# Two-level seven-product queries in the self-attention of a decoder layer

## The chip, the cores and the metric

The kernel runs on one core of one Trainium2 chip. The metric is the device time of one launch in microseconds (us), the median of several runs. A core has a matrix engine (PE, with its weight loads shown apart as PEld), a vector engine (DVE), a scalar engine (ACT), GpSimd (POOL) and a queue engine (SP) that here only issues DMAs. Each works through its own instructions in order; they wait for each other by semaphores.

## The reference

One decoder layer in float32, on x of 32 x 64 x 512, seen as 2048 tokens of 512 features: self-attention against a paged key and value cache, cross-attention against an encoded context, and a linear layer with eight low-rank experts. Each part is added to its input and layer-normalised.

```
x = layernorm(x + self_attention(x, wq, wk, wv, wo, caches, block_idx))
x = layernorm(x + cross_attention(x, context, Wq, bq, Wkv, bkv, Wo, bo))
x = layernorm(x + low_rank_experts(x, W, b, A, B, p_scores))

q = (x @ wq.T) -> 32 heads of 128          # rotary turn, one position for all
keys, values = 512 selected cache rows + 64 new ones, for each of 8 groups
attn = softmax(q . keys / sqrt(128)); out = (attn . values) @ wo.T
```

The change is in `q = x @ wq.T`. Eight key groups of four heads each share keys and values.

## The kernel before

Self-attention walks 128 *units*: key group g (8), token block tb (4 blocks of 512 tokens), head h (4). Four units of one group and block are a *block* b = n // 4; there are 32 blocks. The program order on PE, DVE and ACT is written out by hand; POOL's and SP's is left to a scheduler.

A unit handles four *tiles* i of 128 tokens. `scores` for a tile issues on PE two products of 288 keys each (L834) into one of two buffers; on DVE the row maximum `nmax` (L839); on ACT the exponential with the row sum (L842); on DVE the transposition of the tile before (`turn`, L865), the reciprocal of the sum (L851) and the scaling of p by it (L857; on ACT, L855, in some units). When the four tiles are done, `move` issues 16 DMAs on SP (L877) that bring the transposed p into `pT`. `values` of unit n - 2 (L885) runs on PE inside unit n: in an even unit two chunks, then two; in an odd unit three, then one and a pair of half chunks for both heads (`shared_values`), which ACT copies out (L908).

Between these stand *steps*: seven products q of the next block's queries, and seven products w of an earlier block's output projection. Each matrix of 512 x 512 is cut in four quarters and multiplied by the seven-product scheme (Winograd's form), one level deep: a product is 4 matmuls of 128 x 128 weights against 256 columns (`Product.mul`, L354). Products accumulate in PSUM, in the order 1, 2, 6, 7, 4, 5, 3: one product's sum must be read out of the bank before the next adds to it. The steps of a block stand at places 0 to 3 of its units by this line:

```
steps = {0: "qwqw", 1: "qw q", 2: "wqwq", 3: "w qw"}[h]
```

Place 0 is after the scores of tile 0, place 1 after the first part of `values`, place 2 after the scores of tile 2, place 3 after the second part of `values`. There are eight PSUM banks: two buffers of two banks for the scores, one bank for q, one for w, two for the values. So each q product, whatever its name (x, y, z), goes through the one q bank. ACT copies products 1 and 2 out (L383, L387); DVE adds the five others to the query matrix qT (L372, L395, L399). For w, DVE adds each product to the token sums `acc` (L553); product 1 has a second addition of twice the size (L561). In program order such a reading stands behind the tile's scaling.

POOL makes the operands: `token_sums` for the block's tokens (four subtractions of 128 x 512, L248 to L251), `load_left` for a group's wq (four, L242 to L245), `load_right` for wo (four), `output_sums` for w (four, L325 to L329), and two products of the rotation of the keys. The tokens of each block are loaded again from DRAM as four DMAs of 256 KB on SP (L120), for each of the eight groups.

The cross-attention further down already makes its queries in two levels: 49 products of 128 x 128 weights against 128 columns in two sets, of four and three outer products, 7 inner products each (`DeepQueries`, L493, read out by ACT at L504 to L511 and DVE at L501).

## Time and profile before

| | us |
|---|---|
| runs (three) | 3006.82, 3007.59, 3008.73 |
| median | 3007.59 |
| the profiled execution | 3004.51, of which 3002.7 is the span in the profile |
| PE busy | 2977.4 (99% of the span) |
| DVE busy | 2127.5 (71%) |
| POOL busy | 1218.9 (41%) |
| ACT busy | 1128.1 (38%) |
| granted PE clock | 0.999 of full speed |

The profile page gives busy times of each engine for one execution. A matmul row shows the time of one instruction until its modelled end; since they are pipelined, the rate is read from the distance between starts. One float32 matmul of the program is two PE instructions, so a product of four matmuls is eight. A row of groups gives busy us, mean ns of one, then the idle time of the engine before them and what ended it. The timeline gives the start, the time taken and the operation, runs of equal ones joined as xN.

### The profile page before, as it was taken

To read this page: it belongs to the slowest core of one execution; us is meant where nothing else is said; L and a number is where in the kernel's file an instruction comes from. 1 tells how busy PE (TensorE), PEld (TensorE's weight loads), DVE (VectorE), ACT (ScalarE), POOL (GpSimd) and SP (SyncE) were. 2 spreads that over 40 slices of the span, in tenths; PEclk is the share of its full clock that TensorE was granted. 3 is DMA by queue.
4 is the path that set the end of the run, shared out by engine and by line. 5 is a ranking of instruction groups with operands and counts; after the bars stand their busy time and mean duration, and the time that the engine had idled before them with its cause. 6 is when DMAs were issued, how large, how long until landed. Compare 5 with 4: busy or idle time off the path is not lost.

```text
span 3002.7 us, 46451 instructions
## 1 busy us (share of the span) xinstructions
PE 2977.4 (99%) x16144; PEld 2330.4 (78%) x16144; DVE 2127.5 (71%) x3907; ACT 1128.1 (38%) x2767; POOL 1218.9 (41%) x1024
## 2 busy tenths in 40 slices
PE   8999999999999999999999999999999999999998
PEld 6777777777777777777777768999999999999964
DVE  6787777777787777787787774636656666666686
ACT  4322223223223323323223232334455555555564
POOL 5222322321321321321321223667577577567532
PEclk9999999999999999999999999999999999999999
DMA  6554444444444444444444454666555455445420
GB/s 186 128 131 126 114 115 121 115 115 120 115 115 120 116 114 121 116 114 120 116 115 113 97 124 136 243 247 204 177 179 179 160 183 192 163 160 184 136 81 36
DMA packets 224042, 416.59 MB, mean 139 GB/s; under 512 B 48001, under 2 KB 103425, under 8 KB 215617
## 3 DMA queue, kind: packets, MB, share of 16 engines
q1 hardware_dynamic: 208720, 385.69, 45.0%
q0 software_dynamic: 4304, 19.01, 1.8%
q10 hardware_dynamic: 10784, 8.92, 1.0%
q8 instruction: 130, 2.13, 0.3%
q14 instruction: 104, 0.84, 0.1%
HBM read 206.60 MB, written 33.82 MB: 80 GB/s over the span
## 4 chain that ended last, share of the span: by engine, by line
PE 91%; DVE 3%; POOL 2%; SPq 2%; ACT 1%; DMA 1%; issue 0%; DVEq 0%; ACTq 0%; POOLq 0%
PE po L885 17%; PE s L834 16%; PE sx L1412 2%; PE pox L1495 2%; PE qx_1x L493 2%; PE qx_0x L493 2%; PE qx_2x L493 2%; PE qx_3x L493 2%; PE w_1y L354 1%; PE q_3y L354 1%; PE w_0y L354 1%; PE q_2y L354 1%; PE w_3y L354 1%; PE q_0y L354 1%; PE q_1y L354 1%; SPq L160 1%
## 5 line engine op out<-in xcount | busy, mean ns | idle before, releaser
L842 ACT ACTIVATE p<-s,nmax 128x576 f32<-128x576 f32 x512 | 379.1, 740 | 1210.7 <-DVE nmax L839 1155.4
L834 PE MATMUL s<-kT,qT 128*128 128x288 f32 x2048 | 574.7, 406 | 0.5 <-ACT p L842 0.5
L885 PE MATMUL po<-pT,v 128*128 128x512 f32 (+1 forms) x1280 | 549.0, 602 | 2.4 <-DMA acc<-in_x 1.9
L834 PEld LDWEIGHTS s<-kT,qT 128*128 128x128 f32 x2048 | 387.7, 190 | 100.6 <-issue 17.5
L839 DVE TENSOR_REDUCE nmax<-s 128x1 f32<-128x576 f32 x512 | 384.0, 750 | 58.6 <-PE s L834 57.2
L865 DVE STREAM_TRANSPOSE T<-p 128x576 f32<-128x576 f32 x512 | 394.4, 770 | 12.2 <-ACT p L855 7.4
L885 PEld LDWEIGHTS po<-pT,v 128*128 128x128 f32 (+1 forms) x1280 | 213.4, 189 | 202.0 <-issue 174.8
L857 DVE TENSOR_SCALAR p<-p,den 128x576 f32<-128x576 f32 x488 | 302.0, 619 | 17.1
L325 POOL TENSOR_TENSOR so<-oT,oT 128x512 f32<-128x512 f32 x32 | 40.7, 1272 | 545.3 <-ACT oT L908 545.2
L851 DVE RECIPROCAL den<-den 128x1 f32<-128x1 f32 x512 | 83.9, 164 | 224.8 <-ACT p L842 216.1
L328 POOL TENSOR_TENSOR so<-oT 128x512 f32<-128x512 f32 x32 | 40.7, 1271 | 310.3 <-PE w_1y L354 92.8
L249 POOL TENSOR_TENSOR tx<-xT 128x512 f32<-128x512 f32 x31 | 40.7, 1314 | 199.0 <-PE q_3z L354 63.3
L1444 ACT ACTIVATE exps<-exps,denx 128x64 f32<-128x64 f32 x480 | 121.0, 338 | 0.0
L1515 ACT ACTIVATE oTx<-pox,bv 128x128 f32<-128x128 f32 x248 | 71.1, 490 | 128.3 <-PE pox L1495 128.3
L325 POOL TENSOR_TENSOR sox<-oTx,oTx 128x512 f32<-128x512 f32 x31 | 39.3, 1269 | 149.0 <-DVE oTx L1517 132.4
L535 POOL TENSOR_TENSOR qTx<-d_in 128x512 f32<-128x512 f32 x68 | 85.1, 1274 | 34.7 <-ACT d_in L511 33.3
L842 ACT ACTIVATION_READ_ACCUMULATOR p<-s,nmax 128x1 f32 x512 | 98.7, 193 | 0.0
L535 POOL TENSOR_TENSOR qTx<-d 128x512 f32<-128x512 f32 x60 | 75.1, 1274 | 24.6 <-ACT d L511 23.2
L542 ACT ACTIVATE qTx<-qTx,bq 128x512 f32<-128x512 f32 x128 | 81.9, 713 | 0.0
L1517 DVE TENSOR_SCALAR oTx<-pox,bv 128x128 f32<-128x128 f32 x248 | 70.6, 425 | 14.2 <-PE pox L1495 14.2
L1412 PEld LDWEIGHTS sx<-kv_room,qTx 128*64 128x64 f32 x2048 | 62.3, 138 | 11.1 <-issue 10.1
L908 ACT COPY oT<-po 128x512 f32<-128x512 f32 x128 | 68.2, 587 | 4.1 <-PE po L885 3.8
(590 smaller groups left out, 6217.9 us busy)
## 6 DMA issues: line engine op xcount, KB each, us to landing
pT<-T SPq DMA_DIRECT2D x1016, 80.0 KB
pT<-T SPq DMA_DIRECT2D x1008, 64.0 KB
xT<-tl SPq DMA_DIRECT2D x28, 1792.0 KB
tlb<-tl SPq DMA_DIRECT2D x28, 1344.0 KB
xT<-in_xT SPq DMA_DIRECT2D x123, 256.0 KB
kv_room<-kv SPq DMA_DIRECT2D x32, 512.0 KB
pTx<-Tx SPq DMA_DIRECT2D x256, 64.0 KB
kv<-c SPq DMA_DIRECT2D x28, 512.0 KB
```

What stands on the lines that cost most here:

```text
L354: nc.tensor.matmul(self.banks[b][:, m, :], self.left[i][:, k, m * P : (m + 1) * P], self.right[i][:, k, :], start=(first and m + k == 0), ...
L493: nc.tensor.matmul(o[:, j, :], self.left[s][:, j, LEFT[i], :], self.right[s][:, j, RIGHT[i], :], start=(first and j == 0), stop=(j == len( ...
L535: nc.gpsimd.tensor_tensor(self.q[:, :, i, :, v, :], x.rearrange("p (o u) n -> p o u n", o=2), y.rearrange("p (o u) n -> p o u n", o=2), AL ...
L834: nc.tensor.matmul(s[:, a, :HALF], qTs[n // REP][:, units[n][2], i * P : (i + 1) * P], kTs[g][:, a * HALF : (a + 1) * HALF], start=True, s ...
L839: nc.vector.tensor_reduce(nmax, s[:, :, :HALF], AX.XY, ALU.max, negate=True)
L842: nc.scalar.activation(p.rearrange("q (a k) -> q a k", a=2), s[:, :, :HALF], AF.Exp, bias=nmax, accum_out=den,)
L851: nc.vector.reciprocal(den, den)
L857: nc.vector.tensor_scalar(p, p, den, None, ALU.mult)
L865: nc.vector.transpose(Ts[n][:, :, i, :], ps_.pop((n, i)).rearrange("q (b k) -> q b k", k=SQ))
L885: nc.tensor.matmul(pos[n].rearrange("d (a q) -> d a q", a=NQD), vs[units[n][0]][rows, v, :], pTs[n // 2][rows, :, chunk, :], skip_group_ch ...
L1412: nc.tensor.matmul(s[b * SEQ : (b + 1) * SEQ, i * REP + h, :], qTs[n][:, h, pr * HF + c0 : pr * HF + c0 + SEQ], kvs[n][:, pr, 0, c0 : c0 + ...
L1444: nc.scalar.activation(e[:, k, :], e[:, k, :], AF.Copy, scale=den[:, k : k + 1])
```

## The change

From the second key group on (blocks 4 to 31), the self-attention's queries are made in two levels, as 7 + 7 inner products: set 0 has four outer products (j = 0 to 3), set 1 three. A step of set 0 is four matmuls of 128 x 128 x 128, a step of set 1 three. The operands of the tokens do not depend on the group; POOL makes them once, in the first group, and they are kept in DRAM (`tq_all`) and loaded for every block into the new tile `tq`. The weights of a group are loaded in another layout (`wqD`) into the room of the old operands, and POOL makes the 49 parts of them. Block 0 to 3 keep the old products.

```
-            p = sb.tile([P, NKEY], F32, tag="p", name=f"p{u}", bufs=4)
+            p = sb.tile([P, NKEY], F32, tag="p", name=f"p{u}", bufs=3)
...
-            if n < REP or n >= N - REP and i % 2:
+            if n < REP or i % 2 and (n < 11 or n >= N - REP):
                 nc.scalar.activation(p, p, AF.Copy, scale=den)
...
+        SELF_ORDER = (1, 6, 7, 4, 5, 3, 2)
+            def step(self, s, i):
+                js = 4 - s
+                first = i in (1, 5, 2)
+                if first:
+                    self.bank = bank([P, 4, P], f"{self.name}_{s}{i}", "q")
+                o = self.bank
+                for j in range(js):
+                    nc.tensor.matmul(
+                        o[:, j, :], wdeep[s][:, j, LEFT[i], :], tq[:, RIGHT[i], j, :],
+                        start=(first and j == 0), stop=(j == js - 1), skip_group_check=True,
+                    )
+                k = {1: 0, 6: 1, 7: 3, 4: 2, 5: 3, 3: 1, 2: 0}[i]
+                c, o = self.homes[s][:, :, k, :], o[:, :js, :]
+                if i in (1, 6, 7, 4):
+                    nc.scalar.copy(c, o)
+                else:
+                    reads.append(lambda: nc.vector.tensor_tensor(c, o, c, ALU.add))
+            def post(self, s):
+                g, add, q = nc.gpsimd, ALU.add, self.q
...
+            def query(k):
...
+                    if idx < 14:
+                        s, i = divmod(idx, 7)
+                        dqs[nb].step(s, SELF_ORDER[i])
+                        flush()
+                        if i == 3:
+                            load_tokens(nb + s, 1 - s, 0, slice(4, 7))
+                        if i == 6:
+                            dqs[nb].post(s)
+                            load_tokens(nb + s, 1 - s, slice(1, 4))
...
+            def project(place):
+                if b >= 2 and (h, place) != (1, 1):
+                    w_step(b - 2 if h < 2 else b - 1)
+                    flush()
...
+                scores(n, 0)
+                project(0)
+                scores_first(n, 1)
+                query(0)
+                scores_last(n, 1)
+                values(n - 2, 0, first_half)
+                query(1)
+                scores(n, 2)
+                project(1)
+                scores_first(n, 3)
+                query(2)
+                scores_last(n, 3)
+                values(n - 2, first_half, NKT)
+                if n % 2:
+                    shared_values(n - 2)
+                query(3)
```

`scores_first` ends behind the transposition of the tile before, `scores_last` begins with the reciprocal. In `query`, idx is 4 * h + k, nb is the next block; `post` is four additions of 128 x 512 on POOL after set 0 and three after set 1. So there are two w places and four q places in a unit: q0 after the scores of tile 1, q1 after the first part of the values, q2 after the scores of tile 3, q3 after the second part of the values.

In the first group (units 1 to 10) POOL runs `token_leaves` for each of the four token blocks: a load of 1 MB into the room of `acc[2]`, 12 operations of 128 x 384 or 128 x 512, one store on POOL's queue and six on SP's. The loads of x into `acc[2]` and `acc[3]` move from units 9 to 16 to units 11 to 14, two in each. The order in which the changed program stands on SP at the beginning is: x features for blocks 2 and 3, the stores of token block 0, the load for token block 1, then `move` of units 0 and 1. On POOL the 12 operations of token block 0 stand ahead of its four DMAs for unit 0, those of token block 1 ahead of its four for unit 1.

Gone are, from block 4 on, the 28 reloads of the tokens (four DMAs of 256 KB each), `token_sums` and `load_left`. In their place a block loads 3.2 MB from `tq_all` by six DMAs on SP, and a group five blocks of 256 KB from `wqD`. Once in a group POOL does 8 + 5 operations for the weights. The rotation of a group's keys is issued in two halves.

More of the change, by code (lines that the diff above doesn't have):

```diff
@@ L57, in decoder_layer @@
     xT_in: bass.AP,
+    xD: bass.AP,
+    wqD: bass.AP,
     encT_in: bass.AP,
@@ L687, in decoder_layer @@
         sb = ph.enter_context(tc.tile_pool(name="sa", bufs=2))
+        tqp = ph.enter_context(tc.tile_pool(name="tq", bufs=1))
         begin = ExitStack()
@@ L825, in decoder_layer, with query_block, scores_first @@
         qTs, Ts, pTs, oTs, pos, ps_ = {}, {}, {}, {}, {}, {}
+        def query_block(n, i):
+            q, h = qTs[n // REP], units[n][2]
+            if n < NTB * REP:
+                return q[:, h, i * P : (i + 1) * P]
+            return deep_view(q)[:, HOMES[h % 2, i % 2], 2 * (h // 2) + i // 2, :]
         def scores(n, i):
+            scores_first(n, i)
+            scores_last(n, i)
+        def scores_first(n, i):
             g, tb, h = units[n]
@@ L834, in scores @@
                 nc.tensor.matmul(
-                    s[:, a, :HALF], qTs[n // REP][:, units[n][2], i * P : (i + 1) * P],
+                    s[:, a, :HALF], query_block(n, i),
                     kTs[g][:, a * HALF : (a + 1) * HALF], start=True, stop=True,
@@ L850, in scores, with scores_last @@
                 turn(n, i - 1)
+            ps_[n, i] = p, den
+        def scores_last(n, i):
+            p, den = ps_[n, i]
             nc.vector.reciprocal(den, den)
-            if n < REP or n >= N - REP and i % 2:
+            if n < REP or i % 2 and (n < 11 or n >= N - REP):
                 nc.scalar.activation(p, p, AF.Copy, scale=den)
@@ L968, in flush @@
                 reads.pop(0)()
+        HOMES = {(1, 0): 0, (0, 0): 1, (0, 1): 2, (1, 1): 3}
+        SELF_ORDER = (1, 6, 7, 4, 5, 3, 2)
+        flat = "p a b c -> p (a b c)"
+        wdeep = (
+            wqs.rearrange(flat).rearrange("p (j i n) -> p j i n", j=4, i=7),
+            rooms.rearrange(flat)[:, : 21 * P].rearrange("p (j i n) -> p j i n", j=3, i=7),
+        )
+        spares = [
+            rooms.rearrange(flat)[:, (21 + 4 * i) * P : (25 + 4 * i) * P].rearrange("p (i n) -> p i n", i=4) for i in range(2)
+        ]
@@ new lines, in decoder_layer, with deep_view, run_some @@
+        tq = tqp.tile([P, 7, 4, P], F32, name="tq")
+        tq_all = [[dram.tile([P, 7, n, P], F32, name=f"tq{tb}_{n}") for n in (4, 3)]
+                  for tb in range(NTB)]
+        dself = txs.rearrange(flat).rearrange("p (j k n) -> p j k n", j=4, k=4)
+        def deep_view(q):
+            return q.rearrange("p h t -> p (h t)").rearrange("p (v k n) -> p v k n", v=4, k=4)
+        def run_some(todo, count):
+            for _ in range(min(count, len(todo))):
+                todo.pop(0)()
@@ new lines, in outer_sums, with tt @@
+        def outer_sums(todo, p, left):
+            add = ALU.add
+            def tt(*args):
+                todo.append(lambda: nc.gpsimd.tensor_tensor(*args))
+            if left:
+                tt(p[4], p[0], p[1], sub)
+                tt(p[1], p[1], p[3], add)
+                tt(p[5], p[1], p[0], sub)
+            else:
+                tt(p[4], p[3], p[1], sub)
+                tt(p[1], p[1], p[0], sub)
+                tt(p[5], p[3], p[1], sub)
+            tt(p[6], p[2], p[5], sub)
@@ new lines, in token_leaves, with tt, store @@
+        def token_leaves(tb):
+            raw = acc[2].rearrange("p b (i n) -> p b i n", i=4)
+            more = acc[3].rearrange("p a n -> p (a n)")[:, : 12 * P]
+            more = more.rearrange("p (s b n) -> p s b n", s=3, b=4)
+            r11, r12, r21, r22 = (raw[:, i, :, :] for i in range(4))
+            todo = []
+            def tt(*args):
+                todo.append(lambda: nc.gpsimd.tensor_tensor(*args))
+            y = [tq[:, :, j, :] for j in range(3)]
+            y1, y2, y3 = (v[:, 0:4, :] for v in y)
+            todo.append(lambda: nc.sync.dma_start(
+                out=raw, in_=xD[tb].rearrange("b p (i n) -> p b i n", i=4)
+            ))
+            todo.append(lambda: None)
+            tt(y2, r22, r12, sub)
+            tt(y1, r12, r11, sub)
+            tt(y3, r22, y1, sub)
+            tt(r12, r21, y3, sub)
+            outer_sums(todo, [tq[:, i, 0:3, :] for i in range(7)], False)
+            a, b = tq_all[tb]
+            todo.append(lambda: nc.gpsimd.dma_start(out=a[:, :, 1:4, :], in_=tq[:, :, 0:3, :]))
+            outer_sums(
+                todo, [raw[:, :, i, :] for i in range(4)] + [more[:, i, :, :] for i in range(3)],
+                False,
+            )
+            def store(queue):
+                for dst, src in ((a[:, 0:4, 0, :], r11), (b[:, 0:4, 0, :], r12),
+                                 (b[:, 0:4, 1, :], r21), (b[:, 0:4, 2, :], r22)):
+                    queue.dma_start(out=dst, in_=src)
+                queue.dma_start(out=a[:, 4:7, 0, :], in_=more[:, :, 0, :])
+                queue.dma_start(out=b[:, 4:7, :, :], in_=more[:, :, 1:4, :])
+            todo.append(lambda: None)
+            todo.append(lambda: store(nc.sync))
+            todo.append(lambda: None)
+            todo.append(lambda: None)
+            return todo
@@ new lines, in load_block, with load_first, load_second, first_sums @@
+        def load_block(dst, g, block):
+            nc.sync.dma_start(out=dst, in_=wqD[g, block].rearrange("p (i n) -> p i n", i=4))
+        def load_first(g):
+            load_block(wdeep[0][:, 0, 0:4, :], g, 0)
+            load_block(spares[0], g, 1)
+            load_block(spares[1], g, 3)
+        def load_second(g):
+            load_block(wdeep[1][:, 1, 0:4, :], g, 2)
+            load_block(wdeep[1][:, 0, 0:4, :], g, 3)
+        def first_sums():
+            a, (r12, r22) = wdeep[0], spares
+            a0, a1, a2, a3 = (a[:, j, 0:4, :] for j in range(4))
+            add, todo = ALU.add, []
+            for args in (
+                (a2, a0, r12, sub), (a1, r12, r22, add), (a3, a1, a0, sub), (r12, a1, a0, sub),
+            ):
+                todo.append(lambda args=args: nc.gpsimd.tensor_tensor(*args))
+            outer_sums(todo, [a[:, :, i, :] for i in range(7)], True)
+            return todo
@@ new lines, in second_sums, with load_tokens @@
+        def second_sums():
+            b, todo = wdeep[1], []
+            todo.append(lambda: nc.gpsimd.tensor_tensor(
+                b[:, 2, 0:4, :], b[:, 1, 0:4, :], spares[0], sub
+            ))
+            outer_sums(todo, [b[:, :, i, :] for i in range(7)], True)
+            return todo
+        def load_tokens(b, s, *slots):
+            if NTB <= b < NB:
+                for r in slots:
+                    nc.sync.dma_start(
+                        out=tq[:, r, : 4 - s, :], in_=tq_all[b % NTB][s][:, r, :, :]
+                    )
@@ new lines, in decoder_layer, with __init__ @@
+        class SelfQueries:
+            def __init__(self, b):
+                g, tb, _ = units[b * REP]
+                self.name = f"qd{g}_{tb}"
+                qTs[b] = big.tile([P, REP, TB], F32, tag="qT", name=f"qT{g}_{tb}", bufs=2)
+                self.q = deep_view(qTs[b])
+                self.homes = (dself, self.q[:, 0:3, :, :])
+            def step(self, s, i):
[8 more added lines that the diff above has]
+                        start=(first and j == 0), stop=(j == js - 1), skip_group_check=True,
+                    )
+                k = {1: 0, 6: 1, 7: 3, 4: 2, 5: 3, 3: 1, 2: 0}[i]
+                c, o = self.homes[s][:, :, k, :], o[:, :js, :]
+                if i in (1, 6, 7, 4):
+                    nc.scalar.copy(c, o)
+                else:
+                    reads.append(lambda: nc.vector.tensor_tensor(c, o, c, ALU.add))
+            def post(self, s):
+                g, add, q = nc.gpsimd, ALU.add, self.q
+                d1, d5, d7, d6 = (dself[:, j, :, :] for j in range(4))
+                if s == 0:
+                    g.tensor_tensor(d6, d1, d6, add)
+                    g.tensor_tensor(d7, d6, d7, add)
+                    g.tensor_tensor(q[:, 3, :, :], d7, d5, add)
+                    g.tensor_tensor(d5, d6, d5, add)
+                else:
+                    for v, d in ((1, d1), (2, d5), (0, d7)):
+                        g.tensor_tensor(q[:, v, :, :], q[:, v, :, :], d, add)
@@ L1047, in decoder_layer @@
         short = {0, 1, 2, *range(N - REP, N - 1)}
+        prep, dqs = [], {}
         gathers = {4: 0, 5: 1, 6: 2, 8: 3}
@@ L1057, in decoder_layer @@
                 gather_keys(g + 1, gathers[r])
-            if 0 < n <= PER:
-                b2, j = divmod(n - 1, TPB)
-                nc.scalar.dma_start(out=acc[b2][:, j, :], in_=rows(x, b2)[:, j, :])
+            if 0 < n <= 2 * REP or n in (11, 12, 13, 14):
+                m = 2 * n - 14 if n > 2 * REP else n - 1
+                for m in (m, m + 1) if n > 2 * REP else (m,):
+                    b2, j = divmod(m, TPB)
+                    nc.scalar.dma_start(out=acc[b2][:, j, :], in_=rows(x, b2)[:, j, :])
             if r == 2 * REP and g + 1 < NKV:
@@ L1065, in decoder_layer @@
             if r == 2 * REP + 1 and g + 1 < NKV:
-                rotate(g + 1)
+                rotate(g + 1, 0, NKT // 2)
+                rotate(g + 1, NKT // 2, NKT)
                 later.append(lambda g=g: cached_keys(g + 1))
             b2, k = b + 2, h - (b == 0)
-            if b2 < NB and k in (0, 1):
+            if b2 < NTB and k in (0, 1):
                 if k == 0:
@@ L1106, in spare_bank @@
                     later.pop(0)()
-            scores(n, 0)
-            step(0)
-            spare_bank()
-            scores(n, 1)
-            if n - 1 in short:
-                move(n - 1, (3,), nc.gpsimd)
-            if n >= 2:
-                values(n - 2, 0, 2 if n % 2 == 0 else 3)
-            step(1)
-            scores(n, 2)
-            step(2)
-            if r in gathers and g + 1 < NKV:
-                gather_values(g + 1, gathers[r])
-            scores(n, 3)
-            if n >= 2:
-                values(n - 2, 2 if n % 2 == 0 else 3, NKT)
+            def query(k):
+                nb, idx = b + 1, REP * h + k
+                if nb < NTB:
+                    if (h, k) in ((0, 0), (0, 1), (0, 3), (1, 0), (1, 2), (2, 0), (2, 1)):
+                        q_step(n)
+                        flush()
+                    if idx == 9:
+                        load_first(1)
+                        load_second(1)
+                        prep.extend(first_sums() + second_sums())
+                    if idx == 12:
+                        load_tokens(nb + 1, 0, 0, slice(4, 7), slice(1, 4))
+                elif nb < NB:
+                    if idx == 0:
+                        dqs[nb] = SelfQueries(nb)
+                    if idx < 14:
[7 more added lines that the diff above has]
+                            load_tokens(nb + s, 1 - s, slice(1, 4))
+                            if nb % NTB == NTB - 1 and nb + 1 < NB:
+                                (load_first, load_second)[s](units[n][0] + 1)
+                    if nb % NTB == NTB - 1 and nb + 1 < NB and idx in (8, 15):
+                        prep.extend((first_sums if idx == 8 else second_sums)())
+                run_some(prep, 2 if n < 10 else 1)
@@ new lines, in project @@
+            def project(place):
+                if b >= 2 and (h, place) != (1, 1):
+                    w_step(b - 2 if h < 2 else b - 1)
+                    flush()
+                run_some(prep, 2 if n < 10 else 1)
+            first_half = 2 if n % 2 == 0 else 3
+            if n == 1:
+                prep.extend(part for tb in range(NTB) for part in token_leaves(tb))
+            if n < 2 * REP:
+                scores(n, 0)
+                step(0)
+                run_some(prep, 2)
+                spare_bank()
+                scores(n, 1)
+                if n - 1 in short:
+                    move(n - 1, (3,), nc.gpsimd)
+                if n >= 2:
+                    values(n - 2, 0, first_half)
+                run_some(prep, 2)
+                step(1)
+                scores(n, 2)
+                step(2)
+                run_some(prep, 2)
+                if r in gathers and g + 1 < NKV:
+                    gather_values(g + 1, gathers[r])
+                scores(n, 3)
+                if n >= 2:
+                    values(n - 2, first_half, NKT)
+                    if n % 2:
+                        shared_values(n - 2)
+                run_some(prep, 2)
+                step(3)
+                spare_bank()
+            else:
+                scores(n, 0)
+                project(0)
+                spare_bank()
+                scores_first(n, 1)
+                query(0)
+                scores_last(n, 1)
+                if n - 1 in short:
+                    move(n - 1, (3,), nc.gpsimd)
+                values(n - 2, 0, first_half)
+                query(1)
+                scores(n, 2)
+                project(1)
+                if r in gathers and g + 1 < NKV:
+                    gather_values(g + 1, gathers[r])
+                scores_first(n, 3)
+                query(2)
+                scores_last(n, 3)
+                values(n - 2, first_half, NKT)
@@ L1124, in decoder_layer @@
                 if n % 2:
                     shared_values(n - 2)
-            step(3)
-            spare_bank()
+                query(3)
+                spare_bank()
             if h == REP - 1:
-                if b + 2 < NB:
+                if b + 2 < NTB:
                     g2, tb2, _ = units[(b + 2) * REP]
-                    if tb2 == 0:
-                        wq_cur[g2] = load_left(wqT[:, columns(g2)], f"wq{g2}", nc.gpsimd)
                     tok[b + 2] = token_sums(xTs.pop(b + 2), f"tx{g2}_{tb2}", nc.gpsimd)
@@ L1193, in decoder_layer @@
         wo_cur = {}
-        flat = "p a b c -> p (a b c)"
         wl = (
@@ L1820, with in_blocks @@
     g = {k: np.asarray(a) for k, a in inputs.items()}
+    def in_blocks(a):
+        a = a.reshape(2, 2, P, 2, 2, P)
+        return a.transpose(1, 4, 2, 0, 3, 5).reshape(4, P, 4 * P)
+    feature_major = g["x"].reshape(NTB, P, TPB, DIM).transpose(3, 0, 2, 1).reshape(DIM, NT)
     laid = {
         "x": g["x"].reshape(NT, DIM),
-        "xT": g["x"].reshape(NTB, P, TPB, DIM).transpose(3, 0, 2, 1).reshape(DIM, NT),
+        "xT": feature_major,
+        "xD": np.stack([in_blocks(a) for a in np.split(feature_major, NTB, axis=1)]),
+        "wqD": np.stack([in_blocks(a) for a in np.split(g["L0_attn_wq"].T, NKV, axis=1)]),
         "encT": g["ctx_4096"].reshape(NT, DIM).T,
```

## The prediction

> **What bounds the kernel now.** I read the page's busy times first, then the stages, then one unit in the timeline.

> ```profile
> PE 2977.4 (99%) x16144; PEld 2330.4 (78%) x16144; DVE 2127.5 (71%) x3907; ACT 1128.1 (38%) x2767; POOL 1218.9 (41%) x1024
> ```
> ```profile
> 472.00:700.00 228.00, 228.00 (x894) 163.60 (x893) 177.11 (x318) 66.93 (x156) 61.21 (x50) 1.00 0.47 117
> ```

> The second line is a stretch of one key group, four blocks, in the table by stage (PE, PEld, DVE, ACT, POOL busy, then granted clock, DMA share, GB/s). PE never rests and its clock is full, so here the time is the sum of PE's work, and every wait that is added to PE is paid in full. DVE is at 78%, which hides how late it is at a given moment. The timeline of one unit's beginning (h = 2) shows that:

> ```profile
> 649.96 1.13 PE L834 MATMUL s<-kT,qT 128*128 128x288 f32 x4
> 650.93 1.89 PE L354 MATMUL w_2x<-wo,oT 128*128 128x256 f32 x8
> 651.44 0.74 DVE L839 TENSOR_REDUCE nmax<-s 128x1 f32<-128x576 f32 x1
> 652.28 0.74 ACT L842 ACTIVATE p<-s,nmax 128x576 f32<-128x576 f32 x1 [1.94 <-DVE nmax L839]
> 652.66 1.13 PE L834 MATMUL s<-kT,qT 128*128 128x288 f32 x4
> 652.91 0.19 ACT L842 ACTIVATION_READ_ACCUMULATOR p<-s,nmax 128x1 f32 x1
> 653.12 1.27 POOL L329 TENSOR_TENSOR so<-oT,so 128x512 f32<-128x512 f32 x1
> 653.34 1.36 DVE L857 TENSOR_SCALAR p<-p,den 128x576 f32<-128x576 f32 x1
> 653.63 1.88 PE L885 MATMUL po<-pT,v 128*128 128x512 f32 x4
> 654.62 0.68 DVE L553 TENSOR_TENSOR acc<-w_2x,acc 128x512 f32<-128x512 f32 x1
> 655.22 1.21 DVE L561 TENSOR_TENSOR acc<-w_2x,acc 128x1024 f32<-128x1024 f32 x1
> 656.35 0.74 DVE L839 TENSOR_REDUCE nmax<-s 128x1 f32<-128x576 f32 x1
> ```

> From starts: scores take 0.97 of PE, an old product 1.73, two chunks of values 1.72. DVE's lag d is the start of nmax after the scores' end: tile 1's scores end at 652.66 + 1.13 = 653.79, its nmax starts at 656.35, so d = 2.56. Nobody waits for that today, because the readings of the q bank are far from the next q product.

> The rate of the new products is in the cross-attention, where set 0 and set 1 already exist:

> ```profile
> 2316.45 1.05 PE L493 MATMUL qx_0z<-xT,wq 128*128 128x128 f32 x8
> 2317.34 1.06 PE L493 MATMUL qx_0x<-xT,wq 128*128 128x128 f32 x8
> 2318.23 0.83 PE L493 MATMUL qx_0x<-tlb,wlb 128*128 128x128 f32 x6
> 2318.90 0.83 PE L493 MATMUL qx_0z<-tlb,wlb 128*128 128x128 f32 x6
> 2319.57 1.89 PE L354 MATMUL wx_1x<-xwo,oTx 128*128 128x256 f32 x8
> ```

> A set 0 step takes 0.89 (2316.45 to 2317.34), a set 1 step 0.67.

> **The change, part by part.** *Products.* A block loses 7 x 1.73 = 12.09 and gains 7 x 0.89 + 7 x 0.67 = 10.95 (before rounding): 1.14 saved, times 28 blocks = **-32**. The rows also answer whether weight loads hide behind only 128 columns: 0.89 for eight instructions is 0.11 each, less than one load's 0.19, so loads overlap the matmuls before them. [...]

> *Waits for the q bank, the main term.* Fourteen products instead of seven go through the one bank, and each waits until the one before has been read. The two new pairs q0 to q1 and q2 to q3 have only values between them. PE, counted from where it leaves the scores of the tile before q0 or q2 (T), comes to the next product at T + 0.89 + 1.72 = 2.61 in an even unit (set 1: 2.39), and at T + 3.01 or later in an odd one. The reading: scores' end +0.16, nmax starts 0.04 + d later, exponential 0.84 after it (651.44 to 652.28), the ACT copy 0.86 later (0.64 to the row-sum read, 0.19 for that, 0.03), the copy 0.59 (128 x 384: 0.48), PE again 0.05 later. Sum: 2.54 + d, set 1 2.43 + d. If DVE reads: nmax 0.66 and transposition 0.70 first, then 0.68: 2.29 + d. So PE waits d - 0.07 (set 0, even), d + 0.04 (set 1, even), d - 0.72 (DVE, h = 1, q2 to q3).

> How large is d? DVE needs 2.35 for a tile (nmax 0.66, transposition 0.70 inside the 1.71 until the row sum is there, reciprocal 0.20, scaling 0.44) and 0.60 for a w reading. Between tiles 0 and 1, and 2 and 3, PE takes 1.73 + 0.97 = 2.70 against 2.95: d = 0.28. In unit h = 1 the scores of tiles 2 and 3 are back to back, 0.97 against 2.35: d = 1.42. In unit h = 2 w's product 1 has the second addition, 1.13 more: d = 1.4, or 2.56 as above, where the scaling took 1.36 in place of 0.52 because a POOL operation was running. Waits of a block: q0-q1 and q2-q3 at h = 0, 0.21 each; q2-q3 at h = 1, 0.70; q0-q1 at h = 2, 1.5 to 2.6; q2-q3 at h = 2, 0.32. Each adds some 0.1 for a first load that is not hidden (a product that waited shows 1.99 in place of 1.89). Sum 3.4 to 4.5; more POOL collisions could make it 5.2. I take 4.1: POOL's row of additions (`post`, four, between three of `output_sums`) runs just into tile 0 and 1 of h = 2. Times 28: **+115** (95 to 146). All else in PE's order is far enough apart.

> *POOL.* A block has 4 + 7 operations where it had 4 + 4, at 1.27 each, off the path: q is needed by the next unit, some 5 us after the last reading, the first of three additions takes 1.3 and the first tile needs no more. The 13 operations per group for weights run beside scalings. Scalings beside POOL tensor operations took 0.98 on average, the others 0.52 (from the scaling's and POOL's timeline rows, 103 and 385). Ten hits a group, 0.46 each, seven groups: 32 of DVE's time, of which the bank waits pass on perhaps a third: **+10** (0 to 25). [...]

> *The beginning.* This cannot be read from a row, only bounded. Before, unit 0's moves start on SP at 31.97 and PE takes its values at 42.76, unit 1's at 52.13:

> ```profile
> 31.97 18.26 SPq L877 DMA_DIRECT2D pT<-T  x24
> ```

> In the changed order SP first has to store token block 0, so it waits for POOL. POOL ends the wo sums at 28.9, then has 2 + 1 + 2 operations and eight more (1.27, or 1.00 for 384 columns): about 45. The stores take SP to 47, the next load waits for them to land (48); twelve DMAs at 0.63 end at 56 and land by 58: 15 later than 42.76. Unit 1's last four DMAs stand on POOL behind token block 1, whose load is issued at 48: 53 + 17 of operations + 3 for stores and DMAs + 3 to land = 75.5 against 52.1, less a wait of 1.88 at 64.62 that goes: **+21**. Block 3's stores stand ahead of unit 9's move in the same way, up to 4 more, and the first weights' sums up to 2: **+25** (10 to 40).

> *Edits at nothing.* Three buffers of p: the exponential waits for nmax of its own tile, which DVE runs after the transposition that frees the third buffer. Loads: 2.2 MB more for each block of 56 us is 39 GB/s on 117, so the DMA share goes from 0.47 to about 0.6. SP gets two more DMAs per block at 0.63; it waits 341.9 us for T in 121 units, 2.8 per unit; if that cover were gone, 1.3 a block, 35 in all, inside the range. Scalings put on ACT in units 4 to 10 and x loads in units 11 to 14: inside the 10 to 40. The split rotation: two halves of the same work.

> **Sum.** -32 + 115 + 10 + 25 = +118 on the profiled execution's 3004.5 (span 3002.7 and 1.8 around it) = 3122.5; the median of the runs is 3.1 above that execution, so **3125**. Lower ends: -32 + 95 + 0 + 10 = +73, 3081. Upper: -32 + 146 + 25 + 40 = +179, 3187.

> **Rivals.** *The bank is free in time: faster.* If the readings came through at d of 0.07 or less at the even units, the term of 115 would go and -32 remain, with 0 to 25 for the beginning: 2976 to 3001. It decides at waits under 1.14 us a block. For it: PE waits nowhere in this stage today, and the change moves the q readings ahead of the reciprocal. Against it: ACT's copy at h = 2 comes behind an exponential that comes behind both w additions, at d of 1.4 at the least. *POOL or SP becomes the bound: heavier.* If scores wait for `post`'s additions, or the moves for token loads, by 1.5 us a block, 42 more and the upper terms: over 3195. Against it, SP's 2.8 per unit. *Light waits:* half of 4.1, nothing for POOL, 10 at the beginning, gives 3043 at most. *The products do not get shorter,* for want of hidden loads: 32 more than my forecast, inside the range; the rows at 2316 speak against it.

> **How the numbers follow.** My forecast, 3045 to 3195, 0.80; heavier 0.05; light waits between 3014 and 3045 0.03; within 0.2% (6 us, about what a measurement of this kernel can tell from no change) 0.03; the bank free in time 0.09. Faster 0.09, same 0.03, slower 0.88; the range leaves 0.20 out.

> **What would show it.** Blocks from 4 on should last 59 us in place of 56; PE's rows of waits should name the new step's line with ACT's exponential or copy, or DVE's additions, as releasers, about 4 a block, the largest in units h = 2 at its second step. New steps should start 0.89 and 0.67 apart where they do not wait. The first values should start near 58. If PE shows no waits at the new steps, the main term is wrong; if PE's block is 55, the rival is right.

## The result, and the profile after

The changed kernel takes 3181.13 us (median of four runs, 3178.60 to 3187.64), the kernel before 3007.20 beside it on the same chip: a ratio of 1.0582 (95% interval 1.0564 to 1.0600). It is slower, inside my range, 56 us above the number I named. The profiled execution took 3181.26 with a span of 3179.5, 176.8 more than the span before. Block starts divide that: 54.5 in blocks 0 to 3, 120.1 in blocks 4 to 30 (27 blocks, 4.45 each), 2.2 before the first scores and behind block 30.

The page's busy times, and four blocks of the steady part in the table by stage (columns as for the kernel before):

```profile
PE 3006.6 (95%) x17320; PEld 2352.7 (74%) x17320; DVE 2152.2 (68%) x3949; ACT 1212.8 (38%) x2949; POOL 1465.7 (46%) x1237
```
```profile
527.80:772.70 244.90, 228.59 (x1055) 164.50 (x1053) 181.92 (x324) 77.53 (x182) 87.90 (x73) 0.99 0.56 146
```

Four blocks last 244.9 us instead of 228, PE rests in 16.3 of them, and the granted clock is 0.99 instead of 1.00. Where PE rests, its rows of waits in blocks 4 to 30 say (us in total, times, longest):

```profile
PE qd L1122 <- ACT qT L1129: 69.5, 37, 2.3
PE qd L1122 <- DVE tx L1131: 18.2, 27, 0.7
PE qd L1122 <- ACT tx L1129: 7.0, 15, 1.2
PE po L899 <- DMA pT<-T: 5.6, 4, 1.5
```

The new steps (L1122) wait for the copies (L1129) and additions (L1131) that empty the q bank. The timeline at the worst place, the second step of a unit h = 2:

```profile
1292.47 1.13 PE L846 MATMUL s<-kT,qT 128*128 128x288 f32 x4
...
1293.29 1.29 DVE L871 TENSOR_SCALAR p<-p,den 128x576 f32<-128x576 f32 x1
1293.44 0.83 PE L1122 MATMUL qd<-tq,xT 128*128 128x128 f32 x6
1294.11 1.88 PE L899 MATMUL po<-pT,v 128*128 128x512 f32 x4
...
1294.50 0.68 DVE L555 TENSOR_TENSOR acc<-w_3x,acc 128x512 f32<-128x512 f32 x1
1295.10 1.21 DVE L563 TENSOR_TENSOR acc<-w_3x,acc 128x1024 f32<-128x1024 f32 x1
...
1296.24 0.74 DVE L851 TENSOR_REDUCE nmax<-s 128x1 f32<-128x576 f32 x1
...
1297.07 0.74 ACT L854 ACTIVATE p<-s,nmax 128x576 f32<-128x576 f32 x1 [4.01 <-DVE nmax L851]
1297.71 0.19 ACT L854 ACTIVATION_READ_ACCUMULATOR p<-s,nmax 128x1 f32 x1
1297.81 0.47 ACT L1129 COPY qT<-qd 128x384 f32<-128x384 f32 x1
...
1298.33 0.94 PE L1122 MATMUL qd<-tq,xT 128*128 128x128 f32 x6 [2.34 <-ACT qT L1129]
```

Read it from the end: PE resumes 0.05 after the copy; the copy is behind an exponential, that behind the maximum, and the maximum (1296.24, for scores that ended at 1293.60) behind w's two additions and a scaling that took 1.29 in place of 0.52. PE had been done with step and values at 1295.99. Up to the exponential nothing in this chain is new: the lag of this maximum was 2.46 on average in blocks 4 to 30 before and is 2.53 now. New is that a step waits for what follows it.

What I had not looked for comes right behind such a wait. Another block, PE's rows, then the stage table for the same moments (the seventh number is the granted clock):

```profile
320.08 1.18 PE L1122 MATMUL qd<-tq,xT 128*128 128x128 f32 x6 [2.32 <-ACT qT L1129]
321.05 2.13 PE L846 MATMUL s<-kT,qT 128*128 128x288 f32 x4
322.97 2.42 PE L356 MATMUL w_3x<-wo,oT 128*128 128x256 f32 x8
325.23 1.13 PE L846 MATMUL s<-kT,qT 128*128 128x288 f32 x4
```
```profile
320.00:321.00 1.00, 0.92 (x6) 0.93 (x7) 0.41 (x1) 0.02 (x1) 0.00 (x0) 0.81 0.59 136
321.00:322.00 1.00, 1.00 (x4) 0.73 (x3) 0.00 (x0) 0.48 (x1) 0.00 (x0) 0.50 0.55 128
...
323.00:324.00 1.00, 1.00 (x4) 0.82 (x3) 0.78 (x2) 0.00 (x0) 0.00 (x0) 0.50 0.67 154
324.00:325.00 1.00, 1.00 (x6) 0.88 (x5) 0.73 (x2) 0.83 (x2) 0.00 (x0) 0.98 0.41 94
```

After a rest of 2.3 us PE ran at a granted clock of 0.50 from 320.6 to 324.0: scores took 1.92 from start to start instead of 0.97, and no row shows a wait. That costs 1.7 us more. It does not follow every such wait (the one at 1298.33 is followed at full rate), but 13 of the 27 blocks pay it. The last section shows which.

In the beginning, SP's rows, PE's, and the DMA issues between 36 and 70 us (count, KB each, median us to landing):

```profile
40.36 2.34 SPq L1056 DMA_DIRECT2D tq<-acc  x4
...
45.80 0.40 SPq L1037 DMA_DIRECT2D acc<-in_xD  x1
46.24 24.94 SPq L891 DMA_DIRECT2D pT<-T  x24
```
```profile
46.01 1.13 PE L846 MATMUL s<-kT,qT 128*128 128x288 f32 x4
65.79 3.75 PE L899 MATMUL po<-pT,v 128*128 128x512 f32 x4 [18.65 <-DMA pT<-T]
```
```profile
acc<-in_xD SPq DMA_DIRECT2D x1, 1024.0 KB, 14.1
pT<-T SPq DMA_DIRECT2D x11, 80.0 KB, 7.2
```

The moves start at 46.24 instead of 31.97, and then both their issue and their landing are slow while the stores and the next load are under way. The twelve moves of unit 0 on SP take until 62.98 to issue (SP's row of waits puts 4.6 us of that to the 1 MB load), and the first lands at 60.19, just behind that load, which stands ahead of it on SP and lands at 59.88. The values start at 65.8 instead of 42.8, and again at half rate (3.75 for what takes 1.88, at a granted clock of 0.50).

### The profile page after: what moved, and what is told of

It reads as the page before. It is cut to its first block, busy times and chain, and to the rows that moved or that the text cites. A ratio compares the mean times of both kernels' runs of the same rounds, so it can differ in the third digit from the quotient of the medians.

```text
span 3179.5 us, 49574 instructions
## 1 busy us (share of the span) xinstructions
PE 3006.6 (95%) x17320; PEld 2352.7 (74%) x17320; DVE 2152.2 (68%) x3949; ACT 1212.8 (38%) x2949; POOL 1465.7 (46%) x1237
## 4 chain that ended last, share of the span: by engine, by line
PE 69%; DVE 15%; DMA 6%; ACT 5%; issue 2%; SPq 2%; POOL 1%; DVEq 0%; ACTq 0%; POOLq 0%
PE s L846 10%; PE po L899 9%; PE qd L1122 8%; DVE nmax L851 4%; ACT p L854 3%; DVE p L871 3%; DMA pT<-T 3%; PE sx L1654 2%; PE pox L1737 2%; DVE T L879 2%; DVE acc L555 2%; PE qx_1x L495 2%; SPq L891 2%; PE qx_0x L495 2%; PE qx_2x L495 2%
## 5 line engine op out<-in xcount | busy, mean ns | idle before, releaser
L846 PE MATMUL s<-kT,qT 128*128 128x288 f32 x2048 | 592.1, 415 | 2.1 <-ACT p L854 2.1
L899 PEld LDWEIGHTS po<-pT,v 128*128 128x128 f32 (+1 forms) x1280 | 200.6, 191 | 228.7 <-issue 202.0
L871 DVE TENSOR_SCALAR p<-p,den 128x576 f32<-128x576 f32 x474 | 331.3, 699 | 16.6
L1122 PEld LDWEIGHTS qd<-tq,xT 128*128 128x128 f32 x1176 | 158.5, 195 | 180.4 <-ACT qT L1129 116.1
L1143 POOL TENSOR_TENSOR qT<-qT,tx 128x512 f32<-128x512 f32 x84 | 110.4, 1342 | 370.5 <-DVE qT L1131 370.5
L1137 POOL TENSOR_TENSOR tx<-tx 128x512 f32<-128x512 f32 x28 | 35.6, 1271 | 502.0 <-ACT oT L922 502.0
L1122 PE MATMUL qd<-tq,xT 128*128 128x128 f32 x1176 | 175.4, 287 | 90.7 <-ACT qT L1129 71.8
L1122 PEld LDWEIGHTS qd<-tq,wq 128*128 128x128 f32 x1568 | 202.8, 192 | 78.4 <-ACT tx L1129 42.3
L1122 PE MATMUL qd<-tq,wq 128*128 128x128 f32 x1568 | 212.9, 279 | 11.5 <-ACT tx L1129 7.0
L537 POOL TENSOR_TENSOR qTx<-d_in 128x512 f32<-128x512 f32 x68 | 85.2, 1275 | 34.3 <-ACT d_in L513 33.0
L1129 ACT COPY tx<-qd 128x512 f32<-128x512 f32 x112 | 65.1, 581 | 81.5 <-PE qd L1122 81.5
```

The source lines that it names most:

```text
L537: nc.gpsimd.tensor_tensor(self.q[:, :, i, :, v, :], x.rearrange("p (o u) n -> p o u n", o=2), y.rearrange("p (o u) n -> p o u n", o=2), AL ...
L846: nc.tensor.matmul(s[:, a, :HALF], query_block(n, i), kTs[g][:, a * HALF : (a + 1) * HALF], start=True, stop=True,)
L871: nc.vector.tensor_scalar(p, p, den, None, ALU.mult)
L899: nc.tensor.matmul(pos[n].rearrange("d (a q) -> d a q", a=NQD), vs[units[n][0]][rows, v, :], pTs[n // 2][rows, :, chunk, :], skip_group_ch ...
L1122: nc.tensor.matmul(o[:, j, :], wdeep[s][:, j, LEFT[i], :], tq[:, RIGHT[i], j, :], start=(first and j == 0), stop=(j == js - 1), skip_group ...
L1143: g.tensor_tensor(q[:, v, :, :], q[:, v, :, :], d, add)
```

## The experiments

My theory: PE waits because each step comes to the one q bank before the last reading is through, and what holds the reading up at h = 2 is w's double addition. Rivals: POOL's sums beside DVE, SP's queue with its loads, and for the beginning DMA traffic against POOL's sums. Each time is the median of four runs, of six in the last; "before", run beside each, was 3004.6 to 3005.8, and the ratios are to it. What a place costs is worked out, here and below, from the distances of PE's starts, averaged over blocks 4 to 30 and less the same place before.

**1. w's double addition later.**

```diff
 project:       w_step(b - 2 if h < 2 else b - 1)
-               flush()
+               if (h, place) != (2, 0):
+                   flush()
 ...
                 query(0)
+                flush()
```

> Edit: in units h = 2 the two additions of the output projection's product 1 are put on DVE behind the maximum and the transposition that follow the next scores, instead of ahead of them. Nothing else moves. Main theory (PE waits for the one q bank because its reading stands behind a late exponential): the lag of tile 1 in h = 2 falls from 2.62 to about 0.3 us and the wait at the second product of h = 2 from 2.3-2.9 to about 0.4; 28 blocks times some 2.2 is 62, so 3119 in place of 3181. Rival, POOL collisions: the same additions and POOL operations remain, so 3181 within 6. Rival, the SP queue and its loads: 3181 within 6. If the wait only moves on to the next product of the projection, whose bank those additions set free, the gain is below 20.

Measured 3112.19, ratio 1.0356 (1.0339 to 1.0373): 69 less. The same place:

```profile
1249.36 0.83 PE L1122 MATMUL qd<-tq,xT 128*128 128x128 f32 x6
1250.03 1.88 PE L899 MATMUL po<-pT,v 128*128 128x512 f32 x4
...
1250.41 0.74 DVE L851 TENSOR_REDUCE nmax<-s 128x1 f32<-128x576 f32 x1
...
1251.77 0.65 DVE L555 TENSOR_TENSOR acc<-w_3x,acc 128x512 f32<-128x512 f32 x1
...
1251.98 0.47 ACT L1129 COPY qT<-qd 128x384 f32<-128x384 f32 x1
...
1252.51 0.71 PE L1122 MATMUL qd<-tq,xT 128*128 128x128 f32 x4 [0.60 <-ACT qT L1129]
```

The maximum is ahead of the addition, the wait 0.60. The mean lag is 0.79, not 0.3, because the scaling ahead still takes 1.29. The place gains 1.7 a block; 0.8 more comes from the step itself and the scores and the w product behind it, where nothing at half rate is left. So the lost clock went with the long wait (mean granted clock of the profiled execution 0.992, in the changed kernel 0.986), and the gain was higher than I had reckoned for a shorter wait.

**2. Readings behind the next product.**

```diff
 step:  if i in (1, 6, 7, 4):
-           nc.scalar.copy(c, o)
+           read = lambda: nc.scalar.copy(c, o)
 ...
+       if not first:
+           self.held()
+       if i in (1, 6, 7, 5):
+           self.held = read
+       else:
+           read()
```

> Edit: within a chain of products that add up in one bank (1, 6, 7, 4 and 5, 3) the reading of a product is issued behind the next product, so that PE has no reading to wait for inside a chain; the same instructions run, but a reading takes a sum that is one product too far, so the queries are others. Changes of the chain (h = 1 third to fourth place, h = 2 third to fourth) still wait. Main theory: the waits at h = 0 (0.5 and 0.2) and at the second product of h = 2 (2.3-2.9) go, 3.2 a block, 28 blocks: 90 less, 3091; up to a third of it may come back as waits for the projection's bank. Rivals (POOL collisions, SP and its loads, products that are longer than 0.89 and 0.67): 3181 within 6, since all their work is still there.

Measured 3182.57, 1.0597 (1.0579 to 1.0614): nothing gained. The edit was badly chosen. Product 7 no longer waits for the copy of 6, but for the copy of 1, which now stands on ACT where that of 6 stood; the place costs the same 2.40 a block. It tells nothing apart.

**3. Token preparation on POOL's queue.**

```diff
-            todo.append(lambda: nc.sync.dma_start(out=raw, ...
+            todo.append(lambda: nc.gpsimd.dma_start(out=raw, ...
-            todo.append(lambda: store(nc.sync))
+            todo.append(lambda: store(nc.gpsimd))
```

> Edit: the load and the six stores of each token block's operands are issued by POOL instead of SP, so that SP's queue in the first blocks holds no wait for POOL ahead of the moves. Theory of the beginning (moves stand on SP behind stores that wait for POOL): the values of unit 0 go from 77 us back to some 45, blocks 0 to 3 lose 20 instead of 54.5, so about 3146. Rival (POOL's own row of operations, on which four moves of units 0 to 2 stand, sets the beginning): seven more issues on POOL per token block make it later: 3181 to 3195. The later blocks do not change with either.

Measured 3188.17, 1.0606 (1.0589 to 1.0624): in the rival's range, and no gain. Its reason is not shown by it: POOL's scheduler also took the first sums ahead of the rotation of the keys, so that the first scores began at 31.3 instead of 20.8, while blocks 0 to 3 behind them lasted 255.7 instead of 261.2.

**4. Tokens loaded once.**

```diff
 load_tokens:
-            if NTB <= b < NB:
+            if b == NTB:
```

> Edit: the token operands are read from DRAM for the first deep block alone and stay in SBUF (later blocks and set 1 of most blocks use operands that are not theirs), so SP loses four to five DMAs per block and DRAM 2.2 MB per block. Main theory: SP's moves come on time again, which takes the 1.6 us of late values in one block of four and a few waits for loaded operands: 10 to 20 less in all, 3161 to 3171; the waits for the q bank stay. Rival (SP and the loads are the bound): 60 or more less, under 3120.

Measured 3165.48, 1.0541 (1.0524 to 1.0559): 16 less, as the main theory had it. The late values at the beginning of a unit h = 0 (0.36 a block, 10 us in all) are gone; the bank waits stay. In the profiled execution blocks 4 to 30 are 15 shorter: these 10, and some 7 because only 9 blocks instead of 13 were hit by the half clock, at 1.7 each (last section). SP and its loads are a small part.

**5 and 6. Steps spread, then with the late addition.** Each q step follows its own scores; places 6 and 15 of a block are empty.

```diff
-                scores(n, 0)
-                project(0)
-                scores_first(n, 1)
-                query(0)
+                scores_first(n, 0)
+                query(0)
+                scores_last(n, 0)
+                project(0)
+                scores_first(n, 1)
+                query(1)
...
-                    if idx < 14:
-                        s, i = divmod(idx, 7)
+                    if idx not in (6, 15):
+                        s, i = divmod(idx - (idx > 6), 7)
```

> Edit: the same steps at other places of PE's order. In each unit every q step now follows its own scores (scores, step, product of the projection or values, scores, step and so on) instead of two pairs with only values between, and the places h = 1 third and h = 3 fourth stay empty. Main theory (PE comes to the one q bank before its reading): PE now comes to the next step 3.36 to 3.59 us after the scores ahead of the last step, the copy is done at 2.43 to 2.54 plus DVE's lag, so all waits with a lag under 0.9 go; what stays is tile 1 of h = 2, whose lag of 2.6 from the product with two additions leaves some 1.7. Some 3.2 of a block's waits go, 28 blocks: 90 less, 3091 (3070 to 3115). Rivals (POOL collisions, SP and its loads, longer products) have the same work and stay at 3181 within 10.

Measured 3096.04, 1.0301 (1.0284 to 1.0318): 85 less with the same work, which none of the rivals allows.

> Edit: the places of the run before, and the two additions of the projection's product 1 at h = 2 put on DVE behind the next maximum, as in the first experiment. Main theory: no wait for the q bank is left but some 0.5 a block, so blocks 4 to 30 go from 60.9 to 55.5 to 56.5 us, and the time to 3045 (3025 to 3065). If the additions now hold up the next product of the projection or the values come too late for the moves, 57.5 and 3085.

Measured 3072.11, 1.0219 (1.0202 to 1.0236): 109 less, though 27 short of what I expected. Of four blocks two last 55.97, one 57.86 and the one with the keys' work 58.07. Left at the second step of h = 2 is a wait of 0.7 on average. DVE's scaling shows what feeds it: 179 scalings of 474 stand beside a sum of POOL, 158 in the changed kernel, and such a one takes 1.30 on average instead of 1.06 (first row the changed kernel, second this run):

```profile
L871 DVE TENSOR_SCALAR p<-p,den 128x576 f32<-128x576 f32 x474 | 331.3, 699 | 16.6
```
```profile
L871 DVE TENSOR_SCALAR p<-p,den 128x576 f32<-128x576 f32 x474 | 386.0, 814 | 16.6
```

This is the fastest version that leaves nothing out; it does not reach the kernel before.

**7 and 8. Another beginning, alone and on top of run 6.** The first load on ACT's queue, the others and the stores on POOL's, and all moves of units 0 to 2 on SP:

```diff
+            queue = nc.gpsimd if tb else nc.scalar
...
-        short = {0, 1, 2, *range(N - REP, N - 1)}
+        short = set(range(N - REP, N - 1))
```

> Edit of the beginning alone: the load of the first token block is issued by ACT at its place in unit 1 (so POOL's order can't take its sums ahead of the keys and the projection's weights), the other loads and all stores by POOL, and all moves of units 0 to 2 by SP. Theory: in the third experiment the moves that stood on POOL behind the sums, and the sums that POOL took ahead of the keys, ate what SP gained; with both gone, first values start near 45, blocks 0 to 3 lose 15 to 25 in place of 54.5, and the time is 3150 (3140 to 3160). Rival: the DMA traffic of the stores and of the raw loads (3 MB a token block) holds the moves up on whatever queue they are issued: 3175 to 3190.

Measured 3194.96, 1.0621 (1.0603 to 1.0638).

> Edit: the new places, the late additions and the new beginning together. If the three causes are apart, the gains add: 3181 less 136 less 31 is 3014 (2995 to 3040), about level with the kernel before the change. If they share a cause (a late DVE, a full SP queue), the sum falls short and it stays over 3050.

Measured 3078.66, 1.0241 (1.0224 to 1.0259). Run 7 came out above both of its ranges, and run 8 over 3050, but not for a shared cause: its blocks 4 to 30 last 1536.0, as in run 6 (1534.3). In run 7 block 0 went from 72.3 to 45.1, but block 1 from 57.9 to 103.1, so that blocks 0 to 3 lost 10.6 more than in the changed kernel. Another 9 lie in blocks 4 to 30 of the profiled execution, where the half clock hit 22 blocks instead of 13. PE's rows of waits of run 7:

```profile
PE w_0y L356 <- POOL so L328: 22.3, 1, 22.3
PE po L899 <- ACT qT L385: 12.0, 1, 12.0
PE po L899 <- DMA xT<-in_xT: 10.6, 1, 10.6
```

The first is the projection's operands, which POOL now makes behind the preparation of later token blocks. So the delay was only handed on.

**9. Stores without sums.**

```diff
-            tt(y2, r22, r12, sub)
...
-            outer_sums(todo, [tq[:, i, 0:3, :] for i in range(7)], False)
+            todo.extend(lambda: None for _ in range(8))
...
-                queue.dma_start(out=a[:, 4:7, 0, :], in_=more[:, :, 0, :])
+                queue.dma_start(out=a[:, 4:7, 0, :], in_=raw[:, 0:3, 0, :])
```

> Edit of the beginning of the changed kernel: POOL's sixteen sums per token block are left out and the stores write the loaded features themselves, with the same bytes from the same queues in the same places (so the deep queries are other numbers). SP's queue still holds loads and stores, but no store waits for POOL's sums. If the beginning is late because SP and POOL wait for sums, blocks 0 to 3 lose 5 to 20 instead of 54.5 and the time is 3140 (3130 to 3150). If DMA traffic and the landing of stores before the next load hold the moves up, most of it stays: 3165 to 3181.

Measured 3160.54, 1.0521 (1.0503 to 1.0538): between the two. (The sums left out are twelve per token block, not sixteen, and POOL's one store became two with the same bytes.) Blocks 0 to 3 lose 30.7 instead of 54.5, so about 24 is waiting for POOL's sums; what is left, less the 6 that stay without any preparation (run 10), is about as much for the loads and stores. PE still waits 11.5 for the first moves.

**10. No token preparation.**

```diff
-                        out=tq[:, r, : 4 - s, :], in_=tq_all[b % NTB][s][:, r, :, :]
+                        out=tq[:, r, : 4 - s, :], in_=x4[:, 0 if r == 0 else slice(1, 4), : 4 - s, :]
...
-                prep.extend(part for tb in range(NTB) for part in token_leaves(tb))
+                pass
```

> Edit of the changed kernel: nothing of the token preparation runs; the deep blocks load as many bytes from the features in DRAM (not their operands, so the deep queries are other numbers). This prices the whole beginning: if all of the 54.5 us of blocks 0 to 3 but some 6 (block 3's first deep steps, the weights' sums) is the preparation, 3133 (3125 to 3140). My on-record price for it was 25, which would give 3156.

Measured 3135.04, 1.0432 (1.0415 to 1.0450): the preparation costs 46, and blocks 0 to 3 lose 6.4 without it.

**11. Fewer of POOL's sums.**

```diff
-                    g.tensor_tensor(d6, d1, d6, add)
-                    g.tensor_tensor(d7, d6, d7, add)
                     g.tensor_tensor(q[:, 3, :, :], d7, d5, add)
-                    g.tensor_tensor(d5, d6, d5, add)
-                else:
...
```

> Edit of the changed kernel: of the seven sums on POOL behind each block's steps only the one that writes the fourth quarter remains (so the deep queries are other numbers). By my on-record price POOL's collisions cost 10 us in all, of which this takes less than half: 3177 (3171 to 3181). Rival (the lag of 2.62 at tile 1 of h = 2, and so its bank wait, is POOL's doing: the sums run beside that scaling): the lag falls by up to 1.1, 28 blocks, 15 to 30 less: 3151 to 3166.

Measured 3171.84, 1.0553 (1.0535 to 1.0571): 9 less, at the lower end of my first range; the intervals of the two ratios overlap, so the size is not sure. The lag at tile 1 of h = 2 is 2.55 (2.53 with all sums), so the rival's reason falls. In the trace the wait at the fourth step of h = 2 falls from 0.45 to 0.19 a block, 7 in all.

**12. All causes out.** Runs 6, 10 and 11 in one.

> Edit: the new places and the late additions of the earlier run, no token preparation, and one POOL sum of seven behind each block's steps (the deep queries are other numbers). What is left of the change is the shorter products. If the causes are apart, 3072 less 46 for the preparation less 5 to 10 for POOL's sums is 3019 (3008 to 3028), and blocks without keys' work last under 55.6, below the 55.94 of the kernel before. If the products save nothing, those blocks stay at 55.9 to 56.3 and the time at 3035 or more.

Measured 3015.50, 1.0036 (1.0024 to 1.0049). The sum came out to 4 us; the blocks did not. They last 56.09 to 57.1 (58.22 with keys), not under 55.6. In a block of 56.1 the 98 instructions of the steps would take 10.9 at 0.111 each, 1.2 less than the 56 of the old products (12.1), but the wait at the second step of h = 2 (0.8, with its first load 0.9) and one for the w bank (0.3, with first load 0.4) eat it:

```profile
PE qd L1123 <- ACT qT L1130: 10.7, 21, 0.7
```

## Why the prediction was right, and where it was short

*Products, -32.* Right. Steps start 0.89 and 0.67 apart where they don't wait. 1.2 a block is saved, 32 in 27 blocks. On loads the row decided, 0.11 per instruction against the 0.19 of one load (PEld, L1122), and none exposed where a step doesn't wait.

*Waits for the q bank, +115.* Right in mechanism, place and size. I had 4.1 a block; measured are 4.5, of which 4.0 stands at the steps and 0.5 is small gaps, mostly first loads behind waits. The forecasts of the table hold 0.1 each for such a load, the measured waits don't.

| place | forecast | measured |
|---|---|---|
| h = 0, q0 to q1 | 0.31 | 0.35 |
| h = 0, q2 to q3 | 0.31 | 0.05 |
| h = 1, q2 to q3 | 0.80 | 0.75 |
| h = 2, q0 to q1 | 1.6 to 2.7 | 2.40 |
| h = 2, q2 to q3 | 0.42 | 0.45 |

The step that mattered was to read DVE's lag in the kernel before, where nobody waited for it. Runs 1, 5 and 6 show the cause: the same work in another order gives 69, 85 and 109 us back.

*POOL, +10.* Near in size, as far as the noise lets one say: run 11 gives 9 for six of a block's seven sums, inside the waits of the table. Scalings beside a sum of POOL rose by 55 (103 to 158; I had 70). But I let POOL's sums raise the lag of 2.56, and they do not.

*The price of a wait was the step that was short.* I counted a wait at its length. Behind the wait of 2.3 the granted clock fell to 0.50, too: 0.8 a block at the step, the scores and the w product behind it, 22 us in 27 blocks, in a stage whose clock had always been 1.00. The sum had no term for it. Run 1 shortened the wait and the loss went with it.

*SP's loads at nothing.* Named as a cover of 2.8 a unit with 35 as its price; 10 of that came due. After the change the row of SP's waits for T is 152.9 us in 44 units instead of 341.9 in 121, though another row puts 85.2 in 27 more to DVE's additions, so the cover shrank by less than the first row alone says.

*The beginning, +25 (10 to 40), was mis-sized.* The order was right: POOL's sums ended at 44.7 (forecast 45), the moves started at 46.2 (48). Then I let twelve moves issue in 8 us and land 2 us later; their issue took 17, eleven of them landed after 7.2 (median), and the load for token block 1 took 14.1. First values came at 65.8, not 58, the next unit's at 84.6, not 75.5. Run 10 prices it at 46, above the 40 at which my range for it ended.

*Sum.* Blocks 4 to 30: -32 + 120 + 22 + 10 = 120, against 120.1. Blocks 0 to 3: 54.5, of which 46 is the preparation. With the 2.2 at the ends that is 177. The forecast had 118. It was short by 22 for the clock, 10 for the late values, some 26 for the beginning (54.5 against 25 and block 3's share of 3) and 2 at the ends; the bank waits were 0.4 a block heavier, which is the 10 that it held for POOL. So the main term was forecast; that the total still fell inside the range, with one term over its end and one missing, was luck: the other terms stayed clear of their upper ends. The rival "bank free in time" was wrong by run 1's rows: even with the double addition out of the way a wait of 0.6 stays.

What stays open: how the beginning's 46 could be made to vanish. Runs 3, 7 and 8 only moved it, and a preparation in smaller parts was not tried. Nor was a second bank for q, which might take the wait away; the program has all its eight banks in use. The pure gain of the products, with no wait left, was seen in the steps' rows and never in a block.

## What to carry to other kernels

Before cutting a product into smaller ones that share a bank, read the lag of the engine that empties the bank, at the very place where the next product will stand: a late reading that costs nothing today can become a wait when the product behind it comes sooner (here, behind a lag of 2.46 that nobody had waited for, a wait of 2.40 a block). Spread such steps evenly and put the long reading of another bank behind the short one on the same engine; this gave 109 of 174 us back without any work removed. A preparation "once, at the beginning" cost 46 here, with a DMA share of 0.67 to 0.70 in blocks 0 to 2 against 0.56 in the steady part: count the stores, and the landing of what is queued behind them.

## What the runs showed of the hardware that I had not expected

The 80 KB moves landed three times later beside large DMAs: 7.2 us (median) in the 34 us in which 3.1 MB of stores and a 1 MB load went out, against 2.1 in the page's row for all such moves. The first move landed 0.3 us behind the 1 MB load ahead of it on SP (60.19 and 59.88), in run 9 0.45 behind (45.92 and 45.47). The shared queue is not the whole reason: in run 3 POOL issued the load and the stores, and the 80 KB moves on SP still took 6.7 between 36 and 80 us.

```profile
pT<-T SPq DMA_DIRECT2D x1016, 80.0 KB, 2.1
```
